# Cross-attention and quantized feed-forward on one core: single-pass matmuls for the maximum and the reciprocals in attention

## The chip, the core and the metric

The kernel runs on one NeuronCore of one Trainium2 chip, in one launch. The metric is the device time of the whole program in microseconds (us). Five engines work from queues of their own: TensorE (PE in the profile), VectorE (DVE), ScalarE (ACT), GpSimd (POOL) and SyncE (SP, which here only issues DMAs).

## The reference

A block of 16 batch elements, 512 tokens each, 512 features, 16 heads of 32 features; the context has 120 tokens. Cut to what matters:

```python
x = x + xattn(layernorm(x), ctx, ctx, Wq, Wk, Wv, Wo)
x = x + ffn(layernorm(x), w_gate, w_up, w_down)      # quantized, 1536 hidden features

# xattn, per head
score = rope(q) @ rope(k).T / sqrt(32)               # 512 x 120
attn  = softmax(score, axis=-1)
out   = (attn @ v) ... @ Wo
```

The change touches only the softmax of the attention: the maximum that is taken from every score before the exponential, and the division by the sum after it. The feed-forward part, 1729 us of the span, stays as it is.

## The kernel before

The attention works through the batch elements b = 0 to 15, and in each through four groups g of four heads. Everything is held transposed: `st` has 120 context tokens on the partitions (128 rows with repeats) and for each head 512 query tokens in the free dimension. PE, DVE and ACT carry out their instructions in the order in which the code is written; the order on POOL and SP is chosen by the scheduler that builds the program. A PE bank of PSUM is one of three buffers of the pool `ps_w` (`bank(...)`, tag `w`), handed out in turn: the n-th request can be written only when the readers of request n-3 are done. Two further tiles of two banks each hold `st`, and one bank holds the sums `sm`.

One group g of element b, in the order of the code:

1. `scores` (L329): four matmuls with 32 contraction rows each, one per head, on four row strips of PE. Then DVE takes, per head and token block, the maximum into `mt` (L335).
2. PE makes the queries of the next element (L308, banks) or an output block of the element before (L404).
3. `maxima`: PE transposes `mt` (L345), DVE reduces it to `mx`, 128 x 32 (L347), and spreads it to `nm`, 128 x 512 (L351), with `nrow` (minus one where the token block is the row's own, else zero). Of the 32 rows of a head, only 16 carry something.
4. The DVE part of step 2 follows (`rotate`, L217 and L219, or L410), which frees the bank of step 2.
5. `values` of the group before (L375, L380, then an ACT copy at L384).
6. `exponentials`: four matmuls (L359) of `ones` with `nm` add minus the maximum to `st`, and ACT takes the exponential into `e` (L367), which frees `st` for the next scores.

What is added between the groups: at g = 0 the DVE reduction `largest` of the element two before (L433), `reciprocals` of the element before (L389, DVE) and one more query (`query(1)`); at g = 1 the four `divide` steps (PE matmul L394 of `rep` with the reciprocals, DVE product L398); at g = 2 two output blocks; at g = 3 two more, with transposes for the element two ahead and one block of the gate weights (`WeightBlock`). For b = 1 to 11, except multiples of 4, the keys and values of the next four elements are made too (`go_on`, at g = 0 and g = 1): context transposes for b = 1, 5, 9, values (L258) for b = 2, 6, 10, keys (L267) for b = 3, 7, 11. Elements 4, 8, 12, 13 and 14 have none of this and are called plain below.

The gate weight block of b is read into `wt`, tag `raw_wg`, one buffer (L134); it is quantized at g = 3, and its pieces are written to DRAM by three DMAs (L496): the middle one waits for a POOL subtraction (L171), the last one reads `wt` itself. The next block's read waits for that last DMA.

A float32 matmul stands in the profile as two records, a float32r matmul as one:

```python
t = p2.tile([P, NB, DK], F32, tag="nm", ...)          # L351 writes it
nc.tensor.matmul(st, lhsT=ones[ts(h, DK), :], rhs=nm[ts(h, DK), :], ...)   # L359, float32
nc.tensor.matmul(ps, lhsT=rep[:, g, :], rhs=self.rc[:, part], ...)         # L394, float32
```

Of the kernel before, what the change touches and what calls it, by code (L numbers as in the profile page):

```python
# [9 lines left out]
F32 = mybir.dt.float32  # L10
F32R = mybir.dt.float32r
# [5 lines left out]
ALU = mybir.AluOpType  # L17
AX = mybir.AxisListType
# [3 lines left out]
P = 128  # L22
NH = 16
DK = 32
HG = 4
# [28 lines left out]
def tile_xattn_ffn(  # L54
# [16 lines left out]
    nc = tc.nc  # L71
    B, S, D = x.shape
# [4 lines left out]
    NQ = S // P  # L77
    NG = NH // HG
# [8 lines left out]
    ident = const.tile([P, P], F32, name="ident")  # L87
# [94 lines left out]
    with ExitStack() as at:  # L182
        wpool = at.enter_context(tc.tile_pool(name="at_w", bufs=1))
        p2 = at.enter_context(tc.tile_pool(name="at_2", bufs=2))
# [21 lines left out]
        swap = wpool.tile([P, P], F32, name="swap")  # L206
        nc.sync.dma_start(swap, rope_swap)

        NB = S // DK
# [65 lines left out]
        class Element:  # L275
# [47 lines left out]
            def scores(self, g, kT):  # L323
                b, qT = self.b, self.qs[g]
                self.st = [
                    ps_st.tile([P, 2, S], F32, tag="st", name=f"st_{b}_{g}_{i}") for i in range(2)
                ]
                for h in range(HG):
                    nc.tensor.matmul(  # L329
                        self.st[h // 2][:, h % 2, :], lhsT=kT[ts(h, DK), g, b % BC, :],  # L330
                        rhs=qT[ts(h, DK), :], start=True, stop=True, skip_group_check=True,
                    )
                self.mt = mts[(b * NG + g) % 2]
                for i in range(2):
                    nc.vector.tensor_reduce(  # L335
                        self.mt[:, 2 * i : 2 * i + 2, :NB],
                        self.st[i].rearrange("p h (c j) -> p h c j", j=DK),
                        AX.X, ALU.max, apply_transpose=True,
                    )

            def maxima(self, g):

                nm = f"{self.b}_{g}"
                tp = bank(f"tm_{nm}")[:, :P]
                nc.tensor.transpose(tp, self.mt.rearrange("p h c -> p (h c)"), ident)  # L345
                mx = p2.tile([P, DK], F32, tag="mx", name=f"mx_{nm}")
                nc.vector.tensor_reduce(  # L347
                    mx, tp.rearrange("p (a i) -> p i a", i=DK), AX.X, ALU.max
                )
                t = p2.tile([P, NB, DK], F32, tag="nm", name=f"nm_{nm}", bufs=1)  # L350
                nc.vector.tensor_tensor(  # L351
                    t, mx.unsqueeze(1).to_broadcast([P, NB, DK]),
                    nrow[:, :NB].unsqueeze(2).to_broadcast([P, NB, DK]), ALU.mult,
                )
                self.nm = t.rearrange("p c i -> p (c i)")

# [27 lines left out]
                nc.scalar.copy(self.ao[:, g, :], pv)  # L384

            def reciprocals(self, part=slice(0, S)):
                if part.start == 0:
                    self.rc = p2.tile([P, S], F32, tag="rc", name=f"rc_{self.b}", bufs=1)
                nc.vector.reciprocal(self.rc[:, part], self.sm[:, part])  # L389

            def divide(self, g, part=slice(0, S)):
                n = part.stop - part.start
                ps = bank(f"rp_{self.b}_{g}_{part.start}")[:, :n]
                nc.tensor.matmul(  # L394
                    ps, lhsT=rep[:, g, :], rhs=self.rc[:, part], start=True, stop=True
                )
                ao = self.ao[:, g, part]
                nc.vector.tensor_tensor(ao, ps, ao, ALU.mult)  # L398
# [58 lines left out]
        sign = wpool.tile([P, 1], F32, name="sign")  # L457
        nc.vector.tensor_reduce(sign, swap, AX.X, ALU.add, negate=True)
        pairs = [i ^ 1 for i in range(32)]
        ones = wpool.tile([P, P], F32, name="ones")  # L460
        nc.vector.memset(ones, 1.0)

        row = wpool.tile([P, DK], F32, name="row")
        nc.vector.tensor_reduce(
            row, ident.rearrange("p (h r) -> p r h", r=DK), AX.X, ALU.add
        )
        nrow = wpool.tile([P, DK], F32, name="nrow")
        nc.vector.tensor_scalar(nrow, row, -1.0, None, ALU.mult)

        sel = wpool.tile([P, NG, DK], F32, name="sel")  # L470
        nc.vector.memset(sel, 0.0)
        for g in range(NG):
            nc.vector.memset(sel[:, g, :].rearrange("p (a k) -> p a k", k=NG)[:, :, g], 1.0)

        rep = wpool.tile([P, NG, P], F32, name="rep")
        nc.vector.memset(rep, 0.0)
        for h in range(HG):
            nc.vector.memset(rep[ts(h, DK), :, ts(h, DK)], 1.0)
        for g in range(NG):
            nc.vector.tensor_scalar(rep[:, g, :], rep[:, g, :], row[:, g : g + 1], None, ALU.mult)  # L480

        mts = [wpool.tile([P, HG, DK], F32, name=f"mt{i}") for i in range(2)]
        for t in mts:
            nc.vector.memset(t, 0.0)
        cos_k = wpool.tile([P, SK], F32, name="cos_k")
        sin_k = wpool.tile([P, SK], F32, name="sin_k")

# [40 lines left out]
        for b in range(B):  # L528
            here, nxt, old, older = (el.get(b + i) for i in (0, 1, -1, -2))
            if b + 2 < B:  # L530
                el[b + 2] = Element(b + 2)
            new = el.get(b + 2)
            weight = gate_weight(b - 1) if 1 <= b <= NF else None
            if b % BC == 1 and b // BC + 1 < B // BC:
                keys[b // BC + 1] = Keys(b // BC + 1)
            kvs = keys.get(b // BC + 1)
            for g in range(NG):
                if g == 0:
                    here.attend()
                    if older:  # L540
                        for q in range(3):
                            older.end_normalize(q)
                here.scores(g, keys[b // BC].kT)

                rest = []
                if g < 3:
                    if nxt:
                        rest.append(nxt.query((0, 2, 3)[g]))
                elif old:
                    rest.append(old.output(2))  # L550
                here.maxima(g)
                for f in rest:
                    f()
                if g > 0:
                    here.values(g - 1, keys[b // BC].vt)
                elif old:
                    old.values(NG - 1, keys[(b - 1) // BC].vt)
                here.exponentials(g)

                if weight and g == 1:  # L560
                    weight.load()
                if weight and g == 3:
                    weight.quantize()
                if older and g == 0:
                    older.largest(0)
                    older.end_normalize(3)
                if older and g == 1:
                    for q in range(1, NQ):
                        older.largest(q)
                if new and g == 2:  # L570
                    for q in range(NQ):
                        new.stats(q)
                    for q in range(3):
                        new.normalize(q)
                if b == B - 1:
                    first_tokens(g)

                if g == 0:
                    if old:
                        old.reciprocals()  # L580
                    if nxt:
                        nxt.query(1)()
                if g < 2 and kvs:
                    kvs.go_on(2)
                if g == 1 and old:
                    for i in range(NG):
                        old.divide(i)
                if g == 2 and old:
                    for q in range(2):
                        old.output(q)()  # L590
                if g == 3:
                    if new:
                        new.turn(0)
                        new.normalize(3)
                    if old:
                        old.output(3)()
                        old.end()
                        old.inverse()
                    if new:
                        new.turn(1)  # L600
                    if weight:
                        rest = weight.turn(0)
                    if new:
                        new.turn(2)
                        new.turn(3)
                    if weight:
                        rest()
# [35 lines left out]
    ones = small.tile([2, P], F32, name="ones")  # L643
# [89 lines left out]
    part = lambda t, b, f: t[b, :, :, 2 * f : 2 * f + 2, :]  # L733
# [5 lines left out]
    with ExitStack() as gu:  # L739
# [158 lines left out]
        for b in range(B):  # L898
            for f in range(N2):
                i = b * N2 + f  # L900
# [120 lines left out]
        for k in range(NCH):  # L1021
            i, n = NCH + k, k // N2
            f = k % N2
# [41 lines left out]
            if k == 3:  # L1065
# [8 lines left out]
                low = small.tile([P, 1], F32, name="low")  # L1074
# [15 lines left out]
        while len(multiplied) > 1:  # L1090
# [21 lines left out]
            out=here, in0=elem, scalar=float((P - 1) * NR), in1=here, op0=ALU.mult, op1=ALU.add  # L1112
        )
        row = small.tile([P, 1], mybir.dt.uint32, name="row")
        nc.vector.tensor_tensor(row, here, first_row, ALU.add)
        got = []
        for k, src in (("p", p_d), ("u", u_d)):
            t = small.tile([P, R], F32, name=f"row_{k}")
            nc.gpsimd.indirect_dma_start(
                out=t, out_offset=None,  # L1120
# [9 lines left out]
    with ExitStack() as dn:  # L1130
# [190 lines left out]
        with tc.If(nc.values_load(again[0:1, 0:1], min_val=0, max_val=1)):  # L1321
            every = [(b, h, f) for b, h in units for f in range(0, NF, 4)]
            max_p = small.tile([P, len(every)], F32, name="max_p")
            for i, unit_f in enumerate(every):
                p, _ = factors(*unit_f)
# [4 lines left out]
            for i, unit_f in enumerate(every):  # L1330
                nm = f"all_{i}"
# [71 lines left out]
```

## Time and profile before

| what | value |
|---|---|
| runs | 2711.21, 2714.57, 2718.05 us; median 2714.57 |
| profiled execution | 2716.41 us, its span 2714.6 us |
| mean granted PE clock over the span | 0.979 |
| busy over the span | PE 2586.2, DVE 2067.9, POOL 1603.8, ACT 1092.3 us |
| one plain element (b = 8) | 517.24 to 568.47: 51.23 us |
| b = 9 (contexts) | 568.47 to 623.01: 54.54 us |
| b = 10 (values) | 623.01 to 687.97: 64.96 us |
| b = 11 (keys) | 687.97 to 752.1: 64.13 us |
| L359, one group | 8 records, 1.07 us from their start to the next matmul's |
| L394, one element | 8 records, 3.63 us |

A busy PE counts every matmul from its start to a modelled end, and neighbouring matmuls overlap, so the time of a step is read from start to start: the mean record of L394 is 599 ns, but eight of them pass in 3.63 us. In the timeline a row is start, duration, engine, line, operation, tiles, shapes and count, and in brackets the idle time before it with what ended it.

### The profile page before, as it was taken

What the parts mean: (1) busy time and instruction counts of PE and PEld (TensorE: products, weight loads), DVE (VectorE), ACT (ScalarE), POOL (GpSimd) and SP (SyncE); (2) the same over time, 40 slices, a digit from 0 to 9 for tenths busy, and PEclk for the clock granted to TensorE, in tenths of its full rate; (3) what the DMA queues carried; (4) which work ended last, traced back from release to release, by engine and by line L of the source; (5) the groups of instructions that cost most, each with busy time, mean ns of one, the idle gap of its engine ahead of it and who ended that gap; (6) DMA issues with size and microseconds to landing.
All of it is one profiled execution on the core that took longest, in us unless ns stands there. A gap on an engine that the chain in (4) does not pass through costs nothing. (4 is left out here: it accounts for less than half of the span.)

```text
span 2714.6 us, 30451 instructions
## 1 busy us (share of the span) xinstructions
PE 2586.2 (95%) x10934; PEld 1692.6 (62%) x10934; DVE 2067.9 (76%) x2671; ACT 1092.3 (40%) x1182; POOL 1603.8 (59%) x1011
## 2 busy tenths in 40 slices
PE   8899999999999879999999999999999389999999
PEld 4334434333343347787787878777777278788787
DVE  4667766776777557887878579999998678888886
ACT  1221222222222214444444467766766444444443
POOL 4466665655665145556556147777665367777775
PEclk9999999999999989999999999999999799999999
DMA  4011121111111057666666688888888967777773
GB/s 158 15 62 47 66 89 47 47 54 47 47 68 38 16 202 215 213 194 218 213 198 194 221 296 291 277 276 290 283 279 270 362 236 252 249 255 250 250 248 140
DMA packets 264399, 486.85 MB, mean 179 GB/s; under 512 B 47024, under 2 KB 65584, under 8 KB 264240
## 3 DMA queue, kind: packets, MB, share of 16 engines
q1 hardware_dynamic: 264080, 484.31, 52.7%
q8 instruction: 87, 1.43, 0.2%
q14 instruction: 72, 0.59, 0.1%
q0 software_dynamic: 160, 0.52, 0.0%
HBM read 255.66 MB, written 221.25 MB: 176 GB/s over the span
## 5 line engine op out<-in xcount | busy, mean ns | idle before, releaser
L705 POOL TENSOR_SCALAR oh_d<-oq_d 128x512 fp32r<-128x512 int16 x190 | 398.5, 2119 | 156.1 <-DVE oq_d L1193 155.8
L987 POOL TENSOR_TENSOR po<-gt,t_wu 128x1024 f32<-128x1024 f32 x96 | 231.5, 2411 | 242.6 <-DVE gt L964 127.4
L384 ACT COPY ao<-pv 128x512 f32<-128x512 f32 x64 | 37.5, 586 | 505.3 <-PE pv L375 505.3
L308 PE MATMUL qp<-xnT,wq_sb 128*128 128x512 f32 x512 | 236.4, 604 | 0.0
L404 PE MATMUL op<-wo_sb,ao 128*128 128x512 f32 x512 | 232.1, 601 | 0.0
L792 DVE TENSOR_REDUCE max_g<-t_wg 128x1 f32<-128x1024 f32 x96 | 116.8, 1216 | 135.3 <-ACT t_wg L787 135.3
L705 POOL TENSOR_SCALAR xh_g<-xq_g 128x512 fp32r<-128x512 int16 x60 | 121.6, 2046 | 164.4 <-DMA xq_g<-xi 158.5
L769 PE MATMUL mm_wg<-xm_g,wg 128*128 128x512 f32 x768 | 203.8, 408 | 9.3 <-DMA wg<-wg_d 4.6
L1210 PE MATMUL dn_d<-wd,om_d 128*128 128x512 f32 x768 | 194.6, 402 | 18.2 <-DMA wd<-wd_d 6.4
L725 PE MATMUL mm_wg<-xl_g,wg 128*128 128x512 f32 x768 | 208.0, 393 | 0.0
L725 PE MATMUL mm_wg<-xh_g,wg 128*128 128x512 f32 x768 | 205.7, 390 | 0.0
L220 POOL TENSOR_TENSOR rt_q<-rt_q,sin_q 128x512 f32<-128x512 f32 x64 | 81.4, 1272 | 202.5 <-DVE rt_q L217 202.5
L1193 DVE SCALAR_TENSOR_TENSOR oq_d<-pq_d,r_o,uq_d 128x1024 int16<-128x1024 int16 x96 | 128.0, 1333 | 82.0 <-ACT uq_d L1146 82.0
L725 PE MATMUL mm_wu<-xl_u,wu 128*128 128x512 f32 x672 | 185.8, 398 | 2.2 <-ACT mm_wu L775 2.2
L1210 PE MATMUL dn_d<-wd,ol_d 128*128 128x512 f32 x768 | 184.6, 389 | 0.4 <-ACT dn_d L1222 0.4
L1210 PE MATMUL dn_d<-wd,oh_d 128*128 128x512 f32 x768 | 184.5, 389 | 0.0
L1210 PEld LDWEIGHTS dn_d<-wd,om_d 128*128 128x128 f32 x768 | 144.2, 192 | 63.4 <-DVE om_d L711 20.3
L769 PE MATMUL mm_wu<-xm_u,wu 128*128 128x512 f32 x672 | 173.1, 399 | 11.0 <-ACT t_wu L787 6.8
L335 DVE TRANSPOSE_TENSOR_REDUCE mt<-st 128x32 f32<-128x1024 f32 x128 | 151.7, 1224 | 39.1 <-PE st L329 38.9
L725 PE MATMUL mm_wu<-xh_u,wu 128*128 128x512 f32 x672 | 180.1, 390 | 0.0
L308 PEld LDWEIGHTS qp<-xnT,wq_sb 128*128 128x128 f32 x512 | 92.1, 189 | 137.8 <-issue 111.2
L769 PEld LDWEIGHTS mm_wg<-xm_g,wg 128*128 128x128 f32 x768 | 148.4, 196 | 42.9 <-DVE xm_g L711 8.1
(248 smaller groups left out, 5586.1 us busy)
## 6 DMA issues: line engine op xcount, KB each, us to landing
g_d<-t_wg SPq DMA_DIRECT2D x96, 512.0 KB, 3.4
gt<-g_d SPq DMA_DIRECT2D x96, 512.0 KB, 4.5
u_d<-t_wu SPq DMA_DIRECT2D x96, 512.0 KB, 5.8
p_d<-gt SPq DMA_DIRECT2D x96, 512.0 KB, 5.1
p<-p_d SPq DMA_DIRECT2D x96, 512.0 KB, 4.9
u<-u_d SPq DMA_DIRECT2D x96, 512.0 KB, 5.9
xt<-in_x_dram SPq DMA_DIRECT2D x16, 1024.0 KB, 5.3
x<-xt SPq DMA_DIRECT2D x16, 1024.0 KB, 4.3
```

The lines of the kernel that those rows point to most:

```text
L220: nc.gpsimd.tensor_tensor(v(t), v(t), sin, ALU.mult)
L308: nc.tensor.matmul(ps, lhsT=wq_sb[:, d, ts(g, P)], rhs=self.xnT[:, d, :], start=(d == 0), stop=(d == ND - 1),)
L335: nc.vector.tensor_reduce(self.mt[:, 2 * i : 2 * i + 2, :NB], self.st[i].rearrange("p h (c j) -> p h c j", j=DK), AX.X, ALU.max, apply_tra ...
L384: nc.scalar.copy(self.ao[:, g, :], pv)
L404: nc.tensor.matmul(ps, lhsT=self.ao[:, g, ts(q, P)], rhs=wo_sb[:, g, :], start=(g == 0), stop=(g == NG - 1),)
L705: engine.tensor_scalar(as_runs(p.hi, q), q, TO_256, TO_256, ALU.add, ALU.subtract)
L725: nc.tensor.matmul(ps[:, j, :], lhsT=lhs(j, i)[k], rhs=rhs(j, i)[k], start=(k == 0 and i == 0), stop=(k != 1 and i == n - 1), skip_group_c ...
L769: nc.tensor.matmul(self.ps[:, j, :], lhsT=lhs(j, d), rhs=self.x.p[d].mix, start=(d == 0), stop=(d == ND - 1), skip_group_check=True,)
L792: nc.vector.tensor_reduce(maxes[:, i : i + 1], self.t, AX.XYZ, ALU.max, **how)
L987: nc.gpsimd.tensor_tensor(flat(g.po), flat(g.tile), flat(c.t), ALU.mult)
L1193: nc.vector.scalar_tensor_tensor(out=oq.rearrange("p f t -> p (f t)"), in0=pq, scalar=r_o, in1=uq, op0=ALU.mult, op1=ALU.mult,)
L1210: nc.tensor.matmul(self.ps[j], lhsT=self.p[f // 2].all()[k][:, f % 2, ts(j, P)], rhs=wd.made[f][k], start=(k == 0 and f == 0), stop=(k != ...
```

## The change

The two kinds of matmul become float32r. A value is split into a float32r copy of itself and the remainder, which go to two sets of rows of the same matmul, so that their sum is formed by the contraction.

- `scores`: `mt` has the 16 columns twice; a DVE copy fills the second half (it was zero before).
- `maxima`: `two_halves` makes `hl` from `mx` by a DVE copy to float32r and a DVE multiply-add that leaves the remainder on the rows of the second half; `nm` is made from `hl` in float32r, with `nrow` for all 32 rows of a head.
- `reciprocals`: after the DVE reciprocal, an ACT copy to float32r (`rh`) and a DVE multiply-add on the same tile. `rh` lies in the buffer of tag `raw_wg`, which is that of the gate weight block.
- `divide` multiplies `rep`, now float32r with two rows for each head and group, by `rh`.
- The read of the gate weights moves from g = 1 to g = 2. Of the `largest` reductions of g = 1, two move to g = 2.
- Constants: `ones`, `nrow`, `rep` made anew, `low_m`, `low_r`, `two_rows` added, the clearing of `mt` left out.

```diff
             def scores(self, g, kT):
...
+                nc.vector.tensor_copy(self.mt[:, :, 1, :], self.mt[:, :, 0, :])
             def maxima(self, g):
...
-                t = p2.tile([P, NB, DK], F32, tag="nm", name=f"nm_{nm}", bufs=1)
+                hl = two_halves(p2.tile([P, DK], F32R, tag="mh", name=f"mh_{nm}"), mx, low_m)
+                t = p2.tile([P, NB, DK], F32R, tag="nm", name=f"nm_{nm}", bufs=1)
                 nc.vector.tensor_tensor(
-                    t, mx.unsqueeze(1).to_broadcast([P, NB, DK]),
-                    nrow[:, :NB].unsqueeze(2).to_broadcast([P, NB, DK]), ALU.mult,
+                    t, hl.bitcast(F32).unsqueeze(1).to_broadcast([P, NB, DK]),
+                    nrow.unsqueeze(2).to_broadcast([P, NB, DK]), ALU.mult,
                 )
...
             def reciprocals(self, part=slice(0, S)):
                 if part.start == 0:
                     self.rc = p2.tile([P, S], F32, tag="rc", name=f"rc_{self.b}", bufs=1)
+                    self.rh = p2.tile([P, S], F32R, tag="raw_wg", name=f"rh_{self.b}", bufs=1)
                 nc.vector.reciprocal(self.rc[:, part], self.sm[:, part])
+                two_halves(self.rh[:, part], self.rc[:, part], low_r, nc.scalar.copy)
...
             def divide(self, g, part=slice(0, S)):
...
-                    ps, lhsT=rep[:, g, :], rhs=self.rc[:, part], start=True, stop=True
+                    ps, lhsT=rep[:, g, :], rhs=self.rh[:, part], start=True, stop=True
...
-        ones = wpool.tile([P, P], F32, name="ones")
-        nc.vector.memset(ones, 1.0)
+        ones = wpool.tile([P, P], F32R, name="ones")
+        nc.vector.tensor_scalar(ones, swap, 0.0, 1.0, ALU.mult, ALU.add)
...
+        def two_halves(hl, t, low, copy=nc.vector.tensor_copy):
+            copy(hl, t)
+            nc.vector.scalar_tensor_tensor(
+                out=hl, in0=hl.bitcast(F32), scalar=low, in1=t, op0=ALU.mult, op1=ALU.add
+            )
+            return hl
...
-        rep = wpool.tile([P, NG, P], F32, name="rep")
-        nc.vector.memset(rep, 0.0)
+        rep = wpool.tile([P, NG, P], F32R, name="rep")
         for h in range(HG):
-            nc.vector.memset(rep[ts(h, DK), :, ts(h, DK)], 1.0)
-        for g in range(NG):
-            nc.vector.tensor_scalar(rep[:, g, :], rep[:, g, :], row[:, g : g + 1], None, ALU.mult)
-
-        mts = [wpool.tile([P, HG, DK], F32, name=f"mt{i}") for i in range(2)]
-        for t in mts:
-            nc.vector.memset(t, 0.0)
+            for g in range(NG):
+                nc.vector.tensor_copy(
+                    rep[:, g, ts(h, DK)],
+                    two_rows[:, h, g : g + 1].to_broadcast([P, DK]),
+                )
+        mts = [wpool.tile([P, HG, 2, NB], F32, name=f"mt{i}") for i in range(2)]
...
-                if weight and g == 1:
+                if weight and g == 2:
                     weight.load()
...
-                if older and g == 1:
-                    for q in range(1, NQ):
+                if older and g in (1, 2):
+                    for q in ((1,), (2, 3))[g - 1]:
                         older.largest(q)
```

More of the change, by code (lines that the diff above doesn't have):

```diff
@@ L335, in scores @@
                     nc.vector.tensor_reduce(
-                        self.mt[:, 2 * i : 2 * i + 2, :NB],
+                        self.mt[:, 2 * i : 2 * i + 2, 0, :],
                         self.st[i].rearrange("p h (c j) -> p h c j", j=DK),
@@ L344, in maxima @@
                 tp = bank(f"tm_{nm}")[:, :P]
-                nc.tensor.transpose(tp, self.mt.rearrange("p h c -> p (h c)"), ident)
+                nc.tensor.transpose(tp, self.mt.rearrange("p h k c -> p (h k c)"), ident)
                 mx = p2.tile([P, DK], F32, tag="mx", name=f"mx_{nm}")
@@ L466, in tile_xattn_ffn @@
         )
-        nrow = wpool.tile([P, DK], F32, name="nrow")
-        nc.vector.tensor_scalar(nrow, row, -1.0, None, ALU.mult)
+        nrow = wpool.tile([P, NB], F32, name="nrow")
+        nc.vector.tensor_tensor(nrow, row[:, :NB], row[:, NB:], ALU.add)
+        nc.vector.tensor_scalar(nrow, nrow, -1.0, None, ALU.mult)
+        low_m = wpool.tile([P, 1], F32, name="low_m")
+        nc.vector.tensor_reduce(low_m, row[:, NB:], AX.X, ALU.add, negate=True)
+        low_r = wpool.tile([P, 1], F32, name="low_r")
+        nc.vector.tensor_reduce(
+            low_r, row.rearrange("p (a k r) -> p k a r", k=2, r=NG)[:, 1], AX.XY, ALU.add,
+            negate=True,
+        )
[5 more added lines that the diff above has]
+            return hl
         sel = wpool.tile([P, NG, DK], F32, name="sel")
@@ L473, in tile_xattn_ffn @@
             nc.vector.memset(sel[:, g, :].rearrange("p (a k) -> p a k", k=NG)[:, :, g], 1.0)
-        rep = wpool.tile([P, NG, P], F32, name="rep")
-        nc.vector.memset(rep, 0.0)
+        two_rows = wpool.tile([P, HG, NG], F32, name="two_rows")
+        by_head = ident.rearrange("p (h r) -> p h r", r=DK)
+        nc.vector.tensor_tensor(two_rows, by_head[:, :, :NG], by_head[:, :, NG : 2 * NG], ALU.add)
+        rep = wpool.tile([P, NG, P], F32R, name="rep")
         for h in range(HG):
-            nc.vector.memset(rep[ts(h, DK), :, ts(h, DK)], 1.0)
-        for g in range(NG):
-            nc.vector.tensor_scalar(rep[:, g, :], rep[:, g, :], row[:, g : g + 1], None, ALU.mult)
-        mts = [wpool.tile([P, HG, DK], F32, name=f"mt{i}") for i in range(2)]
-        for t in mts:
-            nc.vector.memset(t, 0.0)
+            for g in range(NG):
+                nc.vector.tensor_copy(
+                    rep[:, g, ts(h, DK)],
+                    two_rows[:, h, g : g + 1].to_broadcast([P, DK]),
+                )
+        mts = [wpool.tile([P, HG, 2, NB], F32, name=f"mt{i}") for i in range(2)]
         cos_k = wpool.tile([P, SK], F32, name="cos_k")
```

## The prediction

> **What bounds the kernel now.** I read the table by stages first, then the timelines of PE, DVE, SP and POOL over one plain element (b = 8).
>
> ```profile
> core 0: us, PE busy (x) PEld busy (x) DVE busy (x) ACT busy (x) POOL busy (x), PEclk, DMA share, GB/s
> 99.60:985.00 885.40, 865.23 (x3605) 342.65 (x3604) 613.09 (x990) 203.09 (x274) 498.23 (x468) 0.99 0.15 52
> 957.50:960.90 3.40, 3.40 (x9) 2.67 (x9) 1.29 (x4) 0.00 (x0) 3.29 (x3) 0.50 0.10 36
> ```
>
> In the attention PE is busy 98% of the time, DVE 69%, DMA 15%: PE sets the pace, with DVE behind it. The third line is a stretch of clock at 0.50, used below.
>
> ```profile
> 523.90 1.14 PE L359 MATMUL st<-nm,ones 32*128 32x512 f32 x8
> 524.97 3.70 PE L308 MATMUL qp<-xnT,wq_sb 128*128 128x512 f32 x8
> 528.61 1.14 PE L329 MATMUL st<-qT,kT 32*128 32x512 f32 x8
> 529.67 3.70 PE L308 MATMUL qp<-xnT,wq_sb 128*128 128x512 f32 x8
> 533.21 0.27 PE L345 MATMUL tm<-ident,mt 128*128 128x128 f32 x1
> ...
> 536.34 3.70 PE L394 MATMUL rp<-rc,rep 128*128 128x512 f32 x8
> ```
>
> No gap on PE. Start to start, L359 takes 1.07 us a group and L394 3.63 us an element. What stands behind PE, and how closely:
>
> ```profile
> 523.74 0.67 DVE L219 TENSOR_TENSOR ra_q<-qp,cos_q 128x512 f32<-128x512 f32 x1
> 524.92 3.35 DVE L389 RECIPROCAL rc<-sm 128x512 f32<-128x512 f32 x1
> 530.02 2.37 DVE L335 TRANSPOSE_TENSOR_REDUCE mt<-st 128x32 f32<-128x1024 f32 x2
> 535.52 0.67 DVE L219 TENSOR_TENSOR ra_q<-qp,cos_q 128x512 f32<-128x512 f32 x1
> ```
>
> The query after L359 (524.97) needs the bank that L219 frees at 524.41: 0.56 us to spare. At g = 1, L394 (536.34) needs the one freed at 536.19: 0.15 us. The transpose at 533.21 needs `mt`, ready at 532.39: 0.8 us.
>
> ```profile
> 527.62 0.38 SPq L496 DMA_DIRECT2D wg_d<-wt_wg  x1
> 530.02 0.33 SPq L134 DMA_DIRECT2D wt_wg<-in_L_ffn_w_gate_dram  x1
> ```
>
> ```profile
> 519.73 6.21 POOL L425 TENSOR_SCALAR xn<-xt,ln_mv,ln_rstd 128x512 f32<-128x512 f32 x3
> ```
>
> The buffer `raw_wg` comes free at about 529.95, when the last weight DMA has landed, 1.7 us after the reciprocal ends (528.27). During `maxima` of g = 0 POOL normalizes without a pause.
>
> **The PE work removed.** Single-pass float32r matmuls 128x512 (L725, 1300.77 to 1301.68) pass four in 0.91 us, 0.23 each, where a float32 one takes 3.63/4 = 0.91. Divides: 4 x 0.23 = 0.91, 2.7 us less an element, 16 elements: 43. L359: float32r on four row strips has no row; side by side as the float32 ones it is about 0.3 us (saves 0.77), one after another 0.91 (saves 0.16). I take 0.3, since L329 and L359 both run their strips side by side; 64 groups x 0.77 = 49. If PE were all that counts: 92 us. It isn't, as the slacks above show.
>
> **The DVE work added, per group.** The copy of `mt`, 128x64, lies between L142 (128x16, 0.17 us) and L489 (128x120, 0.23): 0.2, before the transpose, under its 0.8 us slack. The copy to `hl` and its multiply-add, 128x32: 0.17 each by L142 with 0.04 between dependent instructions, 0.42 in a chain that everything after it in DVE's queue sits behind: `nm`, then L217/L219, which free the bank that PE wants next. So at g = 0, L359 ends 0.77 earlier, but its bank comes free 0.42 later, and of the 0.56 to spare 0.14 is left as the gain. g = 2 has 0.57 to spare and g = 1 too, where `nm` doesn't meet POOL (here it took 1.11, not 0.69): 0.15 each. Only g = 3, where L410 frees the bank 1.2 us early, gains about 0.9 in all. So L359 brings about 1.3 us an element, not 3.1.
>
> **Two prices from the skill.** The DVE copies are one-input float32. L294 on DVE at 43.02 takes 1.11 instead of 0.54 us: POOL's L220 runs until 43.85, and it ends 0.28 after that. The Trainium skill (SBUF — State Buffer, "SBUF: two separate sides") says that DVE in a two-port mode, which float32 copies use, and POOL lock each other out for the whole instruction. POOL's 2.07 us normalizes run at g = 0, where no such DVE instruction stands in the trace. By L142 alone the `hl` copy costs 0.2; by the rule it waits, from about 5.25 to 6.63 on the clock that starts at 517.24. I take the wait, as L294 is the nearest row: then L359 starts at 7.7 and the query at 8.95 instead of 7.73, 1.2 us later. The multiply-add has two inputs from SBUF, as `nm` has, which took 0.69 us in the middle of a normalize at 522.48: no wait.
>
> **The reciprocals.** ACT's copy (L170, 0.63) must wait for the free buffer: with t = time - 517.24, the recip ends at 11.4 (12.8 with the lock), the buffer is free at 12.7, the copy ends at 13.4, the multiply-add (L711, 0.69) at 14.1. DVE stands waiting in between. Behind it: L217, L219 of `query(1)` to 15.4, `mt` of g = 1 to 17.7, its copy to 18.0. PE, which came to the transpose at 15.97, would be there at 15.8 and now waits until 18.0: 2.2 us of idle in a plain element. A gap of 1.97 us (before L394 at 957.25) is followed by 3.4 us at clock 0.50, the third line above; the gaps of 1.25 before L329 at 86.72 and 1.20 at 76.85 were not, each by itself. The skill (TensorE: Matmul & The Clock Gate, "Why this matters for your kernels") puts the limit near 3 us; by it the gap costs 2.2, by the row 2.2 + 3.4/2 = 3.9 at most. I go by the row, with 1.4 for what DVE would not have let PE use anyway. Once g = 1 is late, divides 0.91 instead of 3.63 win it back: scores of g = 2 at 22.5 instead of 22.73 with a full clock, about 23.9 without. DVE's four products (2.7) and the exponentials (L367, 1.94 after L359) allow no more. From there the groups g = 2, 3 gain 0.8.
>
> **The sum by kind of element**, in us gained:
> - plain 4, 8, 12, 13: 0.2 + 0.8 - 1.4 = -0.4 each, -1.6. b = 14 has no weight DMA to wait for: +2.2.
> - contexts 5, 9: the query of g = 1 waits 2.3 for its bank (DVE at 15.4 instead of 12.9), but the 1.23 us wait for a context DMA and the divides give it back: 1.0 + 0.9 - 1.2 = 0.7 each, 1.4. b = 1, without weights: 2.
> - values 2, 6, 10: two value blocks (7 us) after `query(1)` hide the reciprocals. Divides gain 2.5 (ACT's copy of the last block holds a bank for 0.75), g = 1 to 3 gain 0.15 + 0.15 + 0.9, g = 0 0.1: 3.8, less 1.2 for the lock, 2.6 each: 7.8.
> - keys 3, 7, 11: hidden too, but the last rotate (1.35 on DVE) holds a bank: divides gain 1.2, so 2.5 - 1.2 = 1.3: 3.9.
> - b = 0: 1. b = 15 waits on DVE (2.92 idle before L345 at 907.07): added copies against shorter matmuls, 0. The tail: one more copy and multiply-add of 256 columns (0.9) against eight short divides, 0.
>
> Sum: -1.6 + 2.2 + 1.4 + 2 + 7.8 + 3.9 + 1 = 16.7. Constants: some 1.5 us more on DVE before 13.15, where it sits idle 5.67 us for `xt`; 1.5 if that cover goes. The later weight read (2.6 us to land) has from the divides to g = 3, over 15 us; the moved `largest` fill DVE's wait at g = 2. SP: the read of `xt` two ahead could fall behind the later weight read, and would land at about 29 of the 29.8 where it is wanted: 0, at most 1 us an element. After 985 us nothing changes.
>
> The profiled execution took 2716.4 (span 2714.6 and 1.8 around it): 2699.7; against the median of the runs, which is 1.8 lower than that execution, 2697.9. I say 2698.
>
> **Rivals.**
> - PE alone decides: bank waits are shorter than I read them and the copies hide. 92 gained, or 50 and more with part of it: 2623 to 2665. Against it: the 0.15 us of slack at 536.34. Chance 0.10.
> - A wash: clock drops in every element with a 2 us gap for two windows (6.8 us at 0.50, as at 906.3 to 913.1): 7 elements x 1.7 = 12 more lost: 2710. Chance 0.17, with all within 0.3% of 2714.6, about what a measurement of this kernel can tell from no change.
> - Slower by the lock at g = 0: two of the three small DVE instructions each sit out a normalize, not one. Then 2.07 more in the 14 elements from b = 2, 29 us: 2727. With one it is my forecast, with two it is slower. For it: POOL normalizes from t = 2.5 to 8.7 without a gap, and the multiply-add is no `nm`; against it: `nm` itself. Chance 0.23.
> - That the matmuls aren't single-pass or run one strip after another matters little: 0.6 us a group, of which banks hide all but g = 3's (10 us).
>
> **The numbers.** Forecast (8 to 50 gained) 0.50, the others 0.10, 0.17, 0.23: faster 0.60, same 0.17, slower 0.23. The range 2665 to 2730 leaves out the full gain and half of the slower case.
>
> **What would show it.** L359 with 4 records, 0.3 us to the next start, L394 0.9 us a set; L359's follower waiting for DVE's L217/L219; DVE idle before the multiply-add of the reciprocals, then PE idle some 2 us before L345 at g = 1 in plain elements, with the clock at 0.50 behind it; none in b = 2, 3, 6, 7, 10, 11. I am wrong if POOL is put in another order, if the `hl` copy takes 0.2 us among normalizes (7 us better), or if the buffer is free earlier.

## The result and the profile after

The changed kernel takes 2674.69 us (median of 4 runs, 2670.9 to 2677.23), against 2714.38 for the kernel before: a ratio of 0.9852, 95% interval 0.9835 to 0.9869. Measured a second time on another chip, it was 0.9846 (0.9833 to 0.9859). The gain is some 40 us where 16.7 were forecast. The profiled execution took 2674.77 us, its span is 2673.0.

The table by stages of the kernel after, for the whole attention and for three windows of 3.4 us that are used further down:

```profile
core 0: us, PE busy (x) PEld busy (x) DVE busy (x) ACT busy (x) POOL busy (x), PEclk, DMA share, GB/s
99.60:945.00 845.40, 800.48 (x3300) 324.48 (x3300) 649.29 (x1185) 213.54 (x294) 492.39 (x465) 0.98 0.16 54
736.70:740.10 3.40, 3.40 (x18) 1.20 (x11) 2.57 (x6) 1.36 (x2) 1.93 (x2) 0.50 0.03 7
787.90:791.30 3.40, 3.40 (x15) 1.12 (x7) 2.78 (x6) 1.73 (x3) 2.14 (x2) 0.50 0.00 0
512.84:516.24 3.40, 3.40 (x24) 1.22 (x24) 2.94 (x8) 1.29 (x2) 0.79 (x1) 1.00 0.37 144
```

PE is busy 95% of the attention (98% before), DVE 77% (69%). Against the window of the forecast (99.60 to 985.00) PE lost 65 us of busy time, and 25 us more of idle time came in. Where, the timeline of PE shows over the plain element b = 8 (494.93 to 544.85):

```profile
494.93 1.14 PE L329 MATMUL st<-qT,kT 32*128 32x512 f32 x8
...
501.59 0.50 PE L362 MATMUL st<-nm,ones 32*128 32x512 f32 x4
502.02 3.70 PE L308 MATMUL qp<-xnT,wq_sb 128*128 128x512 f32 x8
505.65 1.14 PE L329 MATMUL st<-qT,kT 32*128 32x512 f32 x8
506.73 3.70 PE L308 MATMUL qp<-xnT,wq_sb 128*128 128x512 f32 x8
512.84 0.33 PE L347 MATMUL tm<-ident,mt 128*128 128x128 f32 x1 [2.41 <-DVE mt L340]
...
515.38 1.12 PE L400 MATMUL rp<-rh,rep 128*128 128x512 f32 x3
517.19 0.49 PE L400 MATMUL rp<-rh,rep 128*128 128x512 f32 x1 [0.69 <-DVE ao L404]
517.62 1.14 PE L329 MATMUL st<-qT,kT 32*128 32x512 f32 x8
```

The maximum's four matmuls (now L362) take 0.43 us from their start to the next, 0.64 less than L359 did. At g = 1 PE stands 2.41 us before the transpose, and 0.69 us among the divides (now L400). Behind these, the same element on DVE:

```profile
498.52 0.20 DVE L340 COPY mt<-mt 128x64 f32<-128x64 f32 x1
...
500.17 0.18 DVE L488 CAST mh<-mx 128x32 fp32r<-128x32 f32 x1
500.39 0.25 DVE L489 SCALAR_TENSOR_TENSOR mh<-mh,low_m,mx 128x32 fp32r<-128x32 f32 x1
...
501.92 0.67 DVE L219 TENSOR_TENSOR ra_q<-qp,cos_q 128x512 f32<-128x512 f32 x1
...
503.10 3.34 DVE L394 RECIPROCAL rc<-sm 128x512 f32<-128x512 f32 x1
508.29 0.75 DVE L489 SCALAR_TENSOR_TENSOR rh<-rh,low_r,rc 128x512 fp32r<-128x512 f32 x1 [1.84 <-ACT rh L488]
```

and on SP, ACT and POOL:

```profile
505.28 0.38 SPq L523 DMA_DIRECT2D wg_d<-wt_wg  x1
517.72 0.33 SPq L134 DMA_DIRECT2D wt_wg<-in_L_ffn_w_gate_dram  x1
```

```profile
507.64 0.62 ACT L488 CAST rh<-rc 128x512 fp32r<-128x512 f32 x1 [3.52 <-DMA wg_d<-wt_wg]
```

```profile
497.41 6.20 POOL L431 TENSOR_SCALAR xn<-xt,ln_mv,ln_rstd 128x512 f32<-128x512 f32 x3
```

ACT's copy waits for the weight DMA that was issued at 505.28, DVE waits for the copy, and PE waits for DVE. The small DVE instructions at 498.52 to 500.64 run inside POOL's three normalizes (2.07 us each) at the length they have elsewhere.

Stage by stage, from the starts of `scores` (us):

| stage | b = 8: g = 0 and 1 | g = 2 | g = 3 | b = 10: g = 0 | g = 1 | g = 2 | g = 3 |
|---|---|---|---|---|---|---|---|
| before | 22.73 | 14.80 | 13.70 | 18.24 | 18.22 | 14.80 | 13.70 |
| after | 22.69 | 14.16 | 13.07 | 17.60 | 15.67 | 14.17 | 13.06 |
| gained | 0.04 | 0.64 | 0.63 | 0.64 | 2.55 | 0.63 | 0.64 |

And by kind of element:

| elements | forecast, us gained | measured |
|---|---|---|
| values 2, 6, 10 | 7.8 | 13.4 (4.5 each) |
| keys 3, 7, 11 | 3.9 | 10.4 (3.5 each) |
| plain 4, 8, 12, 13 | -1.6 | 3.3 (1.3, 1.3, 0.26, 0.46) |
| contexts 5, 9 | 1.4 | 5.6 (2.65, 2.97) |
| b = 0 and 1 together | 3 | 2.5 |
| b = 14 | 2.2 | 2.1 |
| b = 15 and the tail | 0 | 0.5 |
| the attention | 16.7 | 37.8 |
| the feed-forward | 0 | 3.8 |

The row of b = 0 and 1 counts from the start of the span. The last line is scatter: in the 15 profiled executions of this study, none of which changes the feed-forward, it took between 1722 and 1731 us. So 21 us of the attention are to be explained.

### The profile page after: what moved, and what is told of

Read it like the earlier page. It is cut to its first block, busy times and chain, and to the rows that moved or that the text cites. A ratio compares the mean times of both kernels' runs of the same rounds, so it can differ in the third digit from the quotient of the medians.

```text
span 2673.0 us, 30019 instructions
## 1 busy us (share of the span) xinstructions
PE 2518.4 (94%) x10610; PEld 1674.4 (63%) x10610; DVE 2107.2 (79%) x2889; ACT 1101.5 (41%) x1199; POOL 1598.2 (60%) x1011
## 5 line engine op out<-in xcount | busy, mean ns | idle before, releaser
L220 POOL TENSOR_TENSOR rt_q<-rt_q,sin_q 128x512 f32<-128x512 f32 x64 | 81.3, 1270 | 192.9 <-DVE rt_q L217 192.9
L814 ACT COPY t_wg<-mm_wg 128x1024 f32<-128x1024 f32 x96 | 97.2, 1012 | 173.5 <-PE mm_wg L752 138.3
```

Of the source, the lines that this page charges most:

```text
L220: nc.gpsimd.tensor_tensor(v(t), v(t), sin, ALU.mult)
L814: nc.scalar.copy(self.t, halves(self.ps))
```

## The experiments

Each ratio is to the kernel before on the same chip, with its 95% interval. The letters in the expectations, in brief: A, what PE saves and doesn't show up is given back at g = 1, where the reciprocals wait for their buffer; B, it is given back in every group by DVE's longer chain; D, formed after the first seven kernels, adds the meeting of small DVE instructions with POOL's products and the place of the `largest` reductions.

**The maximum alone** (`max_only`): reciprocals and divides as before, and the `largest` reductions and the weight read at g = 1.

```diff
-                    ps, lhsT=rep[:, g, :], rhs=self.rh[:, part], start=True, stop=True
+                    ps, lhsT=rep[:, g, :], rhs=self.rc[:, part], start=True, stop=True
...
-                if weight and g == 2:
+                if weight and g == 1:
...
-                if older and g in (1, 2):
-                    for q in ((1,), (2, 3))[g - 1]:
+                if older and g == 1:
+                    for q in range(1, NQ):
```

> The maximum in one pass, the reciprocals and divides as before. Theory A (the bank of the query before is not what the next PE work waits for; each L362 group passes 0.64 us sooner, and PE takes nearly all of it): 64 x 0.64 = 41 us less than before, minus a few where PE waits on DVE: 2675 to 2680, that is nearly the whole of the change. Rival B (bank wait as predicted, 1.3 us an element): about 21 less, 2693.

Measured: 2697.2 us against 2719.92, 0.9924 (0.9905 to 0.9943). Values and keys gained 2.5 us each, four times the 0.64, but a plain element only 1.04 and the context elements lost. The waits of PE in the attention:

```profile
PE tm L347 <- DVE mt L340: 13.5, 9, 3.1
PE tp_c L203 <- DMA ct<-in_ctx_dram: 6.8, 5, 2.9
PE rp L398 <- DVE ao L402: 5.1, 6, 3.6
```

The columns are the sum, how often, and the longest. Much of these sums lies in b = 0 and 15. Elsewhere, with no float32r reciprocals at all, PE still waits in b = 4, 8, 12 and 13 0.41 us each for `mt` and 0.32 for the products behind the three `largest`, and 2.85 and 2.39 us for a context block in b = 5 and 9. A's number failed: the buffer isn't the only place where the gain is given back. The total, 23 us less, is near B's 21, but not by B's cause: values and keys gained twice B's 1.3 us, and the contexts lost.

**The divides alone** (`div_only`): the maximum as before.

```diff
-                nc.vector.tensor_copy(self.mt[:, :, 1, :], self.mt[:, :, 0, :])
...
-                hl = two_halves(p2.tile([P, DK], F32R, tag="mh", name=f"mh_{nm}"), mx, low_m)
-                t = p2.tile([P, NB, DK], F32R, tag="nm", name=f"nm_{nm}", bufs=1)
+                t = p2.tile([P, NB, DK], F32, tag="nm", name=f"nm_{nm}", bufs=1)
...
-        ones = wpool.tile([P, P], F32R, name="ones")
+        ones = wpool.tile([P, P], F32, name="ones")
```

> The reciprocals and divides in one pass, the maximum as before. Theory A: values elements gain 1.9, keys 0.9, contexts some 0.6, plain ones lose 0.6 each (PE waits for mt at g = 1), so 5 to 10 us less than before: 2704 to 2709. Rival B: half of the whole change, about 20 us less: 2694. A loss against before would mean that the stall of DVE at the reciprocals costs more than the divides bring.

Measured: 2704.01 us against 2719.92, 0.9946 (0.9927 to 0.9965). The time lies in A's band, but the kernel before is slower on this chip: 15 us less is between A's 5 to 10 and B's 20. By kind of element the trace is near A: values gained 1.9, keys 0.9, contexts 1.6 (A had 0.6), and plain ones lost 0.3, b = 13 1.0 (A had 0.6). PE waits 17.9 us for `mt`, where it waited 8.7.

**One half only** (`one_half`). It leaves out the remainder of the maximum: no copy of `mt`, no `hl`, no multiply-add; only the float32r part of the maximum is subtracted.

```diff
-                nc.vector.tensor_copy(self.mt[:, :, 1, :], self.mt[:, :, 0, :])
...
-                hl = two_halves(p2.tile([P, DK], F32R, tag="mh", name=f"mh_{nm}"), mx, low_m)
...
-                    t, hl.bitcast(F32).unsqueeze(1).to_broadcast([P, NB, DK]),
+                    t, mx.unsqueeze(1).to_broadcast([P, NB, DK]),
```

> The changed kernel without the remainder of the maximum: the float32r maximum alone is used, so the copy of mt, the copy to hl and its multiply-add are left out (0.2 + 0.42 us of DVE a group). Theory A: nm is ready before PE gets to it, so only the places gain where PE waits for mt: 1 to 4 us less than the changed kernel, 2671 to 2674. Rival B (a bank chain behind DVE): 0.42 x 3 groups x 16 = 20 us less, 2655.

Measured: 2677.41 us, 0.9854 (0.9834 to 0.9873): no different from the change. B falls: three DVE instructions fewer in each of 64 groups bring nothing measurable in the whole, and in the trace the values and keys elements take what they take in the change (60.5 and 60.6 us).

**The same bank** (`same_bank`): the query at g = 1 (`query(1)`) is made to use the bank of `query(0)`, which is what the prediction took for granted.

```diff
-                ps = bank(f"qp_{nm}")
+                if g == 0 and self.b > 0:
+                    self.q0 = bank(f"qp_{nm}")
+                ps = self.q0 if g < 2 and self.b > 0 else bank(f"qp_{nm}")
```

> The changed kernel with query(1) made to use the very bank of query(0), as the prediction took it to do. Theory A (it uses another, free bank): PE waits about 0.6 us for L219 at g = 0 in 15 elements, of which the six with values or keys show all and the others part: 4 to 9 us slower than the changed kernel, 2679 to 2684. Rival B (it is that bank already): no difference, 2675.

Measured: 2683.74 us, 0.9872 (0.9849 to 0.9896). By the ratios that is 2 parts in a thousand (5 us) worse than the change; the intervals overlap. The trace is plainer. The waits of PE:

```profile
PE tm L349 <- DVE mt L342: 21.8, 14, 3.5
PE qp L310 <- DVE ra_q L219: 8.6, 15, 0.7
```

The second row, a wait for L219 in 15 elements, doesn't exist in the changed kernel. There `query(1)` used another bank. Against the change the values elements 6 and 10 lost 0.6 us and the keys 1.0, the plain ones 0.0 to 0.4.

**The buffer freed earlier** (`free_early`): of the three weight DMAs, the one that waits for POOL's subtraction goes last, so that `wt` is read out sooner.

```diff
-                for k, t in enumerate((mix, lo, hf)):
+                for k, t in ((1, lo), (2, hf), (0, mix)):
```

> The changed kernel with the three weight DMAs in another order, the one that reads wt ahead of the one that waits for POOL, so that the buffer of rh is free 8 us sooner. Theory A (the stall in plain and context elements is made by that DMA): ACT's copy starts when the reciprocal ends, DVE idles 0.7 instead of 1.84 us, PE 1.2 us less at L347 of g = 1 in elements 4, 5, 8, 9, 12, 13, and the clock drops of 12 and 13 may go: 7 to 10 us less, 2665 to 2668. Rival C (the DVE work itself makes the stall): no more than 2 us less.

Measured: 2676.15 us against 2714.35, 0.9858 (0.9842 to 0.9875): nothing gained. That is rival C's number, but DVE's own work, which C blames, is not all that holds the stall. Element 8 on DVE, and on POOL:

```profile
510.96 0.79 DVE L489 SCALAR_TENSOR_TENSOR rh<-rh,low_r,rc 128x512 fp32r<-128x512 f32 x1 [0.73 <-ACT rh L488]
...
515.30 1.03 DVE L340 COPY mt<-mt 128x64 f32<-128x64 f32 x1
```

```profile
515.02 1.26 POOL L221 TENSOR_TENSOR qT<-ra_q,rt_q 128x512 f32<-128x512 f32 x1
```

DVE waits 1.1 us less (0.73 for 1.84), and the copy of `mt`, now met by POOL's product, takes 1.03 us instead of 0.19: it ends 0.05 after the product does. PE's gap is 2.18 for 2.41. Against the change b = 4 and 8 gained 0.2 us each; b = 5 lost 2.0, and the clock fell in it.

**The multiply-add later** (`late_low`): ACT's copy stays, the multiply-add of the reciprocals goes behind the rotate of g = 1. `late_free` has both this and the edit before.

```diff
-                two_halves(self.rh[:, part], self.rc[:, part], low_r, nc.scalar.copy)
+                if part.start == 0 and part.stop == S:
+                    nc.scalar.copy(self.rh, self.rc)
...
+                if g == 1 and old:
+                    old.low_halves()
```

> The changed kernel with the multiply-add of the reciprocals moved in DVE's queue from g = 0 to behind the rotate of g = 1, so that DVE doesn't wait for ACT's copy; the DMA order as it is. Theory A: mt of g = 1 is ready when PE comes, the 2.4 us idle of plain elements goes, but then the divides wait for DVE: plain elements gain 1.5 to 1.8, b = 14 and the context elements up to as much, clock drops go: 10 to 14 us less, 2661 to 2665. Rival C (DVE's work, not its wait, is the limit there): at most 3 us less.

> Both of the above. Theory A: the DMA is then hidden behind the moved multiply-add, so the same as the late one alone within 2 us: 2660 to 2664. If the two add up (18 to 22 us less, 2653 to 2657), the buffer still holds something else.

Measured: 2681.54 us, 0.9877 (0.9861 to 0.9894), and with both 2688.57, 0.9901 (0.9884 to 0.9917). Both lose, which neither A nor C had expected. Element 8 of `late_low` on DVE and on PE:

```profile
513.85 0.77 DVE L340 COPY mt<-mt 128x64 f32<-128x64 f32 x1
...
515.37 0.60 DVE L497 CAST mh<-mx 128x32 fp32r<-128x32 f32 x1
...
518.12 1.41 DVE L401 SCALAR_TENSOR_TENSOR rh<-rh,low_r,rc 128x512 fp32r<-128x512 f32 x1
```

```profile
514.67 0.33 PE L347 MATMUL tm<-ident,mt 128*128 128x128 f32 x1 [0.41 <-DVE mt L340]
...
519.67 0.94 PE L409 MATMUL rp<-rh,rep 128*128 128x512 f32 x3 [2.13 <-DVE rh L401]
```

The gap before the transpose is gone (0.41), and one of 2.13 stands before the divides. The three small instructions all meet products of POOL (L220 and L221 at 513.30 to 515.92 and again from 517.71), and each is longer than in the change (0.19, 0.18, 0.75). The clock is 0.50 for 3.4 us right behind (from 521.9), and it falls so in each plain element (in b = 12 for 6.8 us).

**The `largest` reductions moved, in the maximum alone** (`max_moved`): `max_only` with the two reductions at g = 2, as the change has them.

> The maximum in one pass with the divides as before, and now also the two largest reductions moved to g = 2. Theory D (in plain and context elements DVE is the limit between the scores of g = 1 and g = 2, so the moved reductions are part of the gain): 3 to 6 us less than the maximum alone, ratio to before 0.990 to 0.9915. Rival E (they fill idle DVE time either way): same as the maximum alone, 0.9924.

Measured: 2687.96 us against 2716.02, 0.9893 (0.9877 to 0.9909). That is 3 parts in a thousand, 8 us, better than `max_only`, whose interval it just overlaps. In the traces a plain element takes 49.53 us for 50.19, and the wait of 0.32 for the products is gone. A step that the prediction took for free belongs to the gain.

**Three repairs, one after another.** `no_lock_free` is `free_early` with the copy of `mt` on ACT and `hl` made by a second reduction out of PSUM; `mid_low_free` is `free_early` with the multiply-add right behind the rotate of `query(1)`; `all_three` has all of it.

```diff
-                nc.vector.tensor_copy(self.mt[:, :, 1, :], self.mt[:, :, 0, :])
+                nc.scalar.copy(self.mt[:, :, 1, :], self.mt[:, :, 0, :])
...
+                    lambda o, _: nc.vector.tensor_reduce(
+                        o, tp.rearrange("p (a i) -> p i a", i=DK), AX.X, ALU.max
+                    ),
...
                         nxt.query(1)()
+                    if old:
+                        old.low_halves()
```

> The weight DMAs reordered as in free_early, and DVE's two float32 copies[...]: the copy of mt is made by ACT, and hl is made by a second reduction from PSUM. Theory D (the gain of the freed buffer was taken back by the copy of mt standing 0.84 us behind POOL's product L221): mt is ready 1.2 us sooner at g = 1 of elements 4, 5, 8, 9, 12, 13 and the clock drops less: 6 to 9 us less than the changed kernel, ratio to before 0.982 to 0.983. Rival E (the lock is an accident of one element): same as free_early, 0.9858.

> free_early with the multiply-add of the reciprocals directly behind the rotate of query(1) at g = 0: DVE works on the rotate while ACT copies, and POOL is in no product then. Theory D: mt of g = 1 would be 0.7 us sooner than in free_early, but its copy again meets POOL's L220/L221 and waits for their end: 0 to 4 us less than the changed kernel, 0.9840 to 0.9855. Rival E: 6 or more less, below 0.983.

> The three together: DMA order, copies[...], multiply-add behind the rotate. Theory D: PE waits at L347 of g = 1 fall from 2.4 to below 0.6 us in plain elements, the clock drops go, and what is left is DVE's four products before the scores of g = 2: 10 to 13 us less than the changed kernel, ratio to before 0.980 to 0.9815. Rival E (the parts don't add): 0.984 or more.

Measured: 2677.34 us, 0.9856 (0.9841 to 0.9871); 2674.27, 0.9839 (0.9822 to 0.9857); 2670.96, 0.9837 (0.9821 to 0.9852). The second came close to what D gave; the first and the third fell short of it, and `no_lock_free` gave E's number (0.9858). The meeting with the product was no accident, though: the plain elements did get shorter (48.9 us in `no_lock_free`, 48.0 to 48.5 with all three, 49.9 to 51.0 in the change). But b = 5 and 9 went from 51.8 and 51.6 to 54.9 and 55.0 in `no_lock_free`, and to 54.0 and 54.4 with all three. PE of `all_three` in b = 5, and the table by stages just behind:

```profile
344.80 1.83 PE L203 MATMUL tp_c<-ident,ct 120*128 120x120 f32 x8 [2.18 <-DMA ct<-in_ctx_dram]
```

```profile
344.30:351.10 6.80, 5.52 (x20) 3.04 (x20) 2.58 (x4) 1.46 (x3) 0.92 (x1) 0.50 0.36 95
```

PE is early, waits 2.18 us for a context block, and then runs 6.8 us at half its clock. What the plain elements gained went there.

**The contexts read ahead as well** (`all_four`): the third and fourth context block of b = 1, 5 and 9 are read at g = 0, issued from ACT. `after_again` is the change on the same chip.

```diff
+            def fetch(self, i):
+                if i not in self.raw:
+                    ct = p2.tile([SK, D], F32, tag="ct", name=f"ct_{self.c}_{i}")
+                    (nc.scalar if i > 1 else nc.sync).dma_start(ct, cx[self.c * BC + i])
+                    self.raw[i] = ct
...
+                    if g == 0 and b % BC == 1:
+                        for i in (2, 3):
+                            kvs.fetch(i)
```

> all_three with the third and fourth context block of elements 1, 5, 9 read ahead, by DMAs that ACT issues at g = 0 as soon as their buffers are free, so that they don't queue on SP behind the 1 MB read of xt. Theory D (in all_three elements 5 and 9 lost 2.2 to 2.8 us each against the changed kernel, since PE came to their transposes before the data and the clock fell for 6.8 us): the wait of PE for the context DMA goes from 5.5 to below 2 us in all, and 6 to 9 us less than all_three's 0.9837: ratio to before 0.9805 to 0.982. Rival F (the clock falls for PE's other waits there): no change against all_three.

> The changed kernel itself, on the same chip and beside the same runs of before: 0.985, between 0.9835 and 0.987.

Measured: 2664.8 us (2663.14 to 2670.55) against 2718.57, 0.9813 (0.98 to 0.9827), and the change on the same chip 2676.91, 0.9846 (0.9833 to 0.9859). This is the best version, 12 us below the change, as D said. b = 5 and 9 take 49.75 us, the plain elements 48.0 to 48.5, and the row of waits for contexts has shrunk from 5.5 us in `all_three` to

```profile
PE tp_c L203 <- DMA ct<-in_ctx_dram: 1.6, 2, 0.9
```

## Why the prediction was wrong, point by point

The sign and the main new stall were right, the size was not. Three terms of the sum make up the 21 us.

**The bank step failed** ("its bank comes free 0.42 later, and of the 0.56 to spare 0.14 is left as the gain"). In the timelines above `query(1)` starts at 502.02, while L219 reads the bank of `query(0)` until 502.59. So it doesn't wait for L219, and the strict turn of three banks, which the section on the kernel before describes, is not what the program has. The built program says which bank it gets: at g = 0 of b = 8 `query(0)` has bank 2, `tm` bank 0, the values bank 1, and `query(1)` bank 0 again. It needs only L349, which has read `tm` at 500.14. So it is in b = 1 to 14 of both kernels, and the first divide of b = 8 takes the bank of `tm` too. The 0.56 and 0.15 us of "slack" in the profile of before were unrelated times that lay near each other. In the groups that no other stall covers the whole 0.64 arrives: 2.56 us in a values or keys element where I gave 1.3. `same_bank` brings the assumed wait in, 0.57 us in each of 15 elements (8.6 us); `one_half` shows from the other side that the DVE chain which was to hold the bank costs nothing. Divides were the reverse: 2.5 forecast in a values element, 1.9 measured (2.55 - 0.64 at g = 1), and 0.9 for 1.2 in a keys element. Net, with what plain and context elements had from it, this is some 8 of the 21 us. The saving itself was mis-sized as well, 0.64 for 0.77.

**The lock term was wrong** (1.2 us in each of the six values and keys elements, 7.2 in all). The prediction drew it from L294 on DVE, which met POOL's L220, a product of two inputs, and from the rule of the Trainium skill (SBUF — State Buffer, "SBUF: two separate sides"), and applied it to POOL's normalizes, which read one tile. In the kernel after 14 copies of `hl` ran during L431: one took 0.54 us, the others 0.18; 13 copies of `mt` did so at 0.19 to 0.20. Products hold such instructions to their end (all 92 copies and casts of `mt` and `hl` in the traces that began 0.2 us or more ahead of it ended 0.04 to 0.06 behind it): 1.03 and 0.77 us for the copy of `mt`, 0.60 for the cast, in the rows of `free_early` and `late_low`. A normalize holds them only in part, and the 14 traces with these instructions show in which. Of their copies, casts and multiply-adds on DVE that began during a normalize of 2.07 us, all 150 that began less than 0.55 us into it were longer than elsewhere, and none of the 713 that began 0.6 to 1.5 us into it. Those that began after 1.5 us were held to the normalize's end if they were casts (all 23), and not if they were multiply-adds (none of 11). For normalizes the measurement decides against "the whole instruction". The `hl` copy began 0.69 us into its normalize, where the prediction's clock has it too (5.25 against 4.56); that it came 0.1 us behind the part that holds was luck. In b = 13 it began 0.25 us into it:

```profile
824.11 0.54 DVE L488 CAST mh<-mx 128x32 fp32r<-128x32 f32 x1
```

The right figure stood in the prediction as the other bound: "By L142 alone the `hl` copy costs 0.2".

**The clock term was too dear** (1.4 us in four plain elements, and 1.2 in two with contexts, for which the prediction names no cause and which I count here: 8.0 in all). The gap came as forecast, 2.41 us for 2.2, but the clock fell behind it only in b = 12 and 13: the windows at 736.70 and 787.90 stand at 0.50, the one at 512.84, behind the 2.41 us gap of b = 8, at 1.00. Those two elements gained 0.26 and 0.46 instead of 1.3: 1.9 us paid, 6.1 too much charged. A row of before (1.97 us, clock 0.50) was taken as what always happens; the limit near 3 us that the skill gives (TensorE: Matmul & The Clock Gate, "Why this matters for your kernels") is no better here. The traces show what tells the four apart. Within each trace all falls of the clock lie whole multiples of 3.413 us apart, within 2 ns (in the change 736.66, 787.86 and 869.78 are 15 and 24 of them apart), so what counts is how much idle time lies between two such instants. The stretches before the falls of b = 12 and 13, then those of b = 4 and 8 with the most idle time:

```profile
733.25:736.66 3.41, 1.18 (x13) 0.47 (x17) 2.86 (x6) 0.00 (x0) 1.70 (x2) 1.00 0.84 302
784.45:787.86 3.41, 1.40 (x13) 0.56 (x17) 2.85 (x7) 0.01 (x1) 1.48 (x2) 1.00 0.89 308
286.10:289.51 3.41, 1.45 (x4) 0.38 (x2) 3.41 (x6) 0.00 (x0) 3.01 (x3) 1.00 0.52 106
511.38:514.79 3.41, 1.95 (x17) 0.56 (x17) 2.85 (x9) 0.56 (x1) 1.00 (x1) 1.00 0.80 288
```

PE was idle for 2.23, 2.01, 1.96 and 1.46 us of them: the gaps of b = 4 and 8 are cut in two. In the attention of the 15 traces, at full clock, 2.0 us or more in one stretch was always followed by a fall, less than 1.2 never; between these both occur. The stretches lie otherwise in each execution. In the profile of `after_again`, the same kernel, b = 4, 12 and 13 are hit (2.42, 2.18 and 1.91 us). By these figures I estimate that a gap of 2.41 us has about an even chance to hold 2.0 in one stretch; the prediction charged every element 1.4 us.

**The reciprocals were right.** The copy on ACT waits for the weight DMA and ends at t = 13.33 (forecast 13.4), the transpose starts 17.91 after the element does (forecast 18.0), `scores` of g = 2 at 22.69 (22.5). b = 14, which has no weight to wait for, gained 2.1 (2.2). What this wait costs was not what a look at it suggests, though: freeing the buffer earlier moved `mt` into a product of POOL and gained nothing.

**Where the rest of the saved PE work is.** 64 groups of 0.64 and 16 elements of 2.7 are 84 us; 38 arrived in the attention. In the traces' sums of waits, PE now waits for `mt` 24.7 us where it waited 8.7, for DVE's products 8.0 where it waited 2.0, and for the keys' rotate 2.9 where it waited none:

```profile
PE tm L347 <- DVE mt L340: 24.7, 11, 3.8
PE rp L400 <- DVE ao L404: 8.0, 10, 2.5
PE rp L400 <- DVE ra_k L219: 2.9, 3, 1.0
```

These are the kernel after's; each `<-` names the instruction that PE waited for. They account for 25 us. The other 21 are no row: PE's busy time fell by 65 us, not by 84. Most of that can be read. The four divides of an element no longer follow one another closely (in b = 8 they start at 515.38, 515.73, 516.00 and 517.19), and in b = 1 to 15 they keep PE busy for 1.4 to 2.0 us, not 0.91: 12 us. And the clock stood at 0.50 for 27.4 us of the attention's window, before for 17.3: at half speed that is 5 us. For the few that are left I have no account.

**The rivals.** PE alone (2623 to 2665) was too much, for the waits just named. The wash by the clock and the slowdown by the lock both rested on the two terms that failed. That `all_four` reaches 2664.8 shows how much of the first rival could be had.

## What to carry to other kernels

Before pricing a wait for a buffer, look whether the later instruction in the trace ever starts while the supposed holder still reads: one overlap disproves the wait, and a small positive slack proves nothing. When a row is used to price contention, match both partners, also the other engine's kind of instruction, its number of inputs, and where in it the meeting falls. And a gap taken away on the pacing engine can come back at the next thing that is nearly late: here three repairs of plain elements went into two waits for contexts, and only with the fourth did they pay.

## What of the hardware was unexpected

- GpSimd's two-input products hold small copies and casts on DVE to their end (copy 0.19 to 1.03, cast 0.18 to 0.60 us) and lengthen the 128x512 multiply-add (0.75 to 1.41). Its one-input normalizes of 2.07 us do so in their first 0.55 us (150 of 150) and not between 0.6 and 1.5 us (none of 713). This is read from rows that lie side by side; no kernel tested the pair by itself.
- Four float32r matmuls on four row strips pass in 0.43 us, where eight float32 records took 1.07.
- The clock falls only at instants 3.413 us apart, and the same gap of 2.4 us is followed by the half clock or not, by how much of it (2.0 us or more: always) lies between two of them. What decides between 1.2 and 2.0 us, and whether the half clock lasts 3.4 or 6.8 us, as behind the 2.18 us of `all_three`, stays open.
